# Earlier projections and adjacency reloads in four column parts, in a one-core graph kernel

## The chip, the cores and the metric

One core of one Trainium2 chip. Its engines are named as the profile names them: PE (TensorE, matmuls), PEld (TensorE's weight loads), DVE (VectorE), ACT (ScalarE), POOL (GpSimd) and SP (SyncE, which here only issues DMAs). Time is device time in microseconds (us). Lower is better.

## The reference

Two layers on 4096 nodes with 512 features. What matters of it:

```python
# layer 0
a = adj + eye(4096)
d = sum(a, axis=1) ** -0.5
out = relu((d[:, None] * a * d[None, :]) @ x @ W.T + b)
x = layernorm(x + out)
# layer 1: 8 heads, key size 64
q, k, v = x @ Wqs, x @ Wks, x @ Wvs            # per head
scores = q @ k.T / 8 + 0.01 * eye - 1e16 * (1 - max(adj, eye))
att = softmax(scores)
x = layernorm(x + sum over heads of (att @ v) @ Wo)
```

The adjacency matrix is 4096 x 4096 in float32 (64 MB). An off-diagonal entry is present with a chance of about 1/512, the diagonal is always present, and every present value is between 0.05 and 1.

## The kernel before, in words

Because all edges are below one and few, the kernel uses a short way: the mask of layer 1 leaves each node only itself, so layer 1 becomes one product with a combined weight `wvo`, and layer 0 becomes a gather over the few edges of a row. A test at the end (L1224) decides whether the short way held; if not, a general kernel follows. Only the short way, `few_edges_below_one`, runs here.

The rows are cut into NT = 32 tiles of 128. The work has two phases.

**Phase 1** (loop at L1049, steps t = 0 to 32) reads every adjacency tile once.

- SP loads adjacency tile t+3 (`load_first`, L561; `load_a`, L541). 14 tiles are "early" (0, 1, 3, 5, ... 25) and go with tiles 27 to 31 ("resident") into the pool `big` of five buffers `a_t`. The other 13 ("again": 2, 4, ... 26) pass through two buffers `a_n` and have to be read a second time in phase 2.
- ACT sums the rows of tiles that are not early (`sum_rows`, L710), or looks for negative entries in early ones (`sum_negative`, L715). POOL makes the degree factor `d_all` from the sum (`scaling`, L722 to L725).
- The projection x @ W.T of a tile: POOL issues the load of `x_t` (L550, five loads ahead, six buffers), PE transposes it (L689), ACT copies the transpose to `xT` (L694), PE multiplies with `wT` (`times`, L703) into one of five PSUM buffers `acc`. When the degree is known, ACT scales it (`keep_y`, L736) and POOL stores it to `y` in DRAM (L738).
- DVE scans adjacency tiles for their edges: per tile eight segments of 512 columns, each with one L752 (MAX8, the eight largest) and one L753 (their places). The function `some` (L986) advances this scan nine of its sixteen steps a tile per t. The order of tiles is early, resident, again (L560). Edges found are sorted (L756 to L838) and matched into nine slots (L844 to L900, with small steps on PE, ACT and DVE).

A list `due` (L1027 to L1032) holds, for each tile, the step in which `keep_y` runs. Step t begins with the projections whose due step lies between `lo` and `hi`:

```python
lo, hi = t + 1 + (t > EARLIER), t + 1 + (t >= EARLIER)      # L1058, EARLIER = NT - 7
ahead = [j for at, j in due if lo <= at <= hi]
```

So a projection runs one step ahead of its `keep_y`, and two steps ahead from t = 25 on.

**Phase 2** (loop at L1280) runs over output tiles i in the order of L560, nine slots k each.

- POOL gathers one row of `y` per node and slot (`gather`, L1110, an indirect DMA of 256 KB), 18 gathers ahead (L1099), in 19 buffers. The first gather needs all of `y`.
- For i > 0 the first two gathered buffers are added up by ACT (L1127) and DVE (L1129), called the presum below. PE multiplies each gathered buffer with a small matrix (L1316), nine products for i = 0 and eight for most others.
- DVE makes `h` from the result (`scaled`, L1180, and `residual`, L1188), which frees `yo` and `x_t` for the next `load_own` (L1115, SP). PE transposes `h` and multiplies it with `wvo`; ACT and DVE normalise it; ACT stores it (L1220).
- Between these, DVE scans the remaining tiles, shared out evenly (L1327). A tile of "again" is read a second time by `reload` (L994), called at k = 8 when a buffer is free: ACT must have looked through the old tile for negatives (`scan_half`, L1153, one half at k = 3 and one at k = 8) and DVE must have scanned it.

The order of the instructions on each engine is not the order of these lines: a scheduler reorders them. Only copies marked by `keep_in_program_order` (L696, L735) stay. Each engine, and SP's queue of DMA issues, then runs in its fixed order and waits in place.

Of the kernel before, what the change touches and what calls it, by code (L numbers as in the profile page):

```python
# [419 lines left out]
def few_edges_below_one(  # L420
# [21 lines left out]
    NT = N // P  # L442
# [33 lines left out]
    p1 = first.enter_context(tc.tile_pool(name="first", bufs=2))  # L476
# [64 lines left out]
    def load_a(t, pool=big, name="a_t", parts=1):  # L541
        a_t = pool.tile([P, N], FP, name=name)
        for c in range(parts):
            o = ts(c, N // parts)
            nc.sync.dma_start(a_t[:, o], adj[ts(t, P), o])
        return a_t
# [14 lines left out]
    def load_first(t, parts=1):  # L561
        if t in early or t in resident:
            return load_a(t, parts=2 if t == NT - 1 else parts)
        return load_a(t, pn, "a_n")

    a_tiles = {0: load_first(0, 4)}
# [8 lines left out]
    wT = p1.tile([P, ND, D], FP, name="wT", bufs=1)  # L575
# [25 lines left out]
    def load_second_weights():  # L601

        nc.sync.dma_start(
            wv.rearrange("p (h f) -> p h f", h=H),
            wvs.rearrange("h (p j) k -> p h (j k)", j=ND),
        )
        su1 = p1.tile([P, 2, ND, D], FP, name="wo", bufs=1)
        nc.sync.dma_start(su1[:, 0], wo.rearrange("(r a) k o -> (a k) r o", a=2))
        return su1

    def order_second_weights():
        nc.gpsimd.tensor_copy(
            w_nat.rearrange("p j (h k) -> p j h k", h=H),
            wv.rearrange("p (h j k) -> p j h k", h=H, j=ND),
        )
# [70 lines left out]
    def transpose_rows(src, dcs=range(ND)):  # L686
        pt = ps_t.tile([P, 512], FP, name="pt")
        for dc in dcs:
            nc.tensor.transpose(pt[:, ts(dc, P)], src[:, ts(dc, P)], ident)  # L689
        return pt  # L690

    def evacuate(pool, name, pt, pinned=False):
        dst = pool.tile([P, ND, P], FP, name=name, bufs=2)
        copy = nc.scalar.copy(dst.rearrange("p c s -> p (c s)"), pt[:, :D])  # L694
        if pinned:
            tc.keep_in_program_order(copy)  # L696
        return dst

    def times(srcT, w, u=None, dcs=range(ND)):
        if u is None:  # L700
            u = ps_a.tile([P, D], FP, name="acc")
        for dc in dcs:
            nc.tensor.matmul(  # L703
                u, srcT[:, dc, :], w[:, dc, :], start=(dc == 0), stop=(dc == ND - 1)
            )
        return u

    def sum_rows(dst, part):
        dump = wk_.tile([P, N], mybir.dt.uint8, name="dump")
        nc.scalar.activation(dump[:, : part.shape[1]], part, AF.Copy, accum_out=dst)  # L710

    def sum_negative(t, a_t, halves=(0, 1)):
        dump = wk_.tile([P, N], mybir.dt.uint8, name="dump")
        o = slice(halves[0] * N // 2, (halves[-1] + 1) * N // 2)
        nc.scalar.activation(  # L715
            dump[:, o], a_t[:, o], AF.Relu, scale=-1.0,
            accum_out=neg_all[:, t, halves[0] : halves[0] + 1],
        )

    def scaling(t, more=None):  # L720
        deg = small.tile([P, 1], FP, name="deg")
        nc.gpsimd.tensor_scalar(deg, deg_all[:, t : t + 1], 1.0, None, op0=ALU.add)  # L722
        if more is not None:
            nc.gpsimd.tensor_tensor(deg, deg, more, ALU.add)
        nc.gpsimd.tensor_tensor(d_all[:, t : t + 1], deg, mhalf, ALU.pow)  # L725

    def keep_y(t, u):
        if t in due_first:
            y_t = p1.tile([P, D], FP, name="y_t", bufs=4)
        else:  # L730
            if not y_bank:
                y_bank.append(p1.tile([P, 8, D], FP, name="wo", bufs=1))
            y_t = y_bank[0][:, y_count[0] % 8]
            y_count[0] += 1
        tc.keep_in_program_order(  # L735
            nc.scalar.activation(y_t, u, AF.Copy, scale=d_all[:, t : t + 1])  # L736
        )
        nc.gpsimd.dma_start(y[ts(t, P), :], y_t)  # L738
# [172 lines left out]
    def match(*stages):  # L911
        for stage in stages:
            n = staged[stage]
            if stage == KEY:
                ready = n < len(sorted_)
            elif stage == PERM:
                ready = n < staged[RANKS] and n - staged[MOVE] < 2
            else:
                ready = n < staged[stage - 1]
            if stage == ACROSS:  # L920
                ready = ready and n == staged[RANKS]
            if stage == MOVE:
                ready = ready and n == staged[END]
            if not ready:
                continue
            t = order[n]
            e = edges[t]
            if stage == KEY:
                e["key"] = match_key(t)
            elif stage == ACROSS:  # L930
                e["pk"] = match_across(e["key"])
            elif stage == RANKS:
                e["rank"] = match_ranks(e["key"], e["pk"])
            elif stage == PERM:
                e["perm"] = match_perm(e["rank"])
            elif stage == MOVE:
                e["pm"] = match_move(e["rec"], e["perm"])
            else:
                match_end(t, e["pm"])
                matched.add(t)  # L940
            staged[stage] += 1
# [44 lines left out]
    def some(upto):  # L986
        while count[0] < upto:
            count[0] += 1
            next(work, None)
# [4 lines left out]
    def reload():  # L994

        t = queue.pop(0)
        reloaded.append(t)
        a_tiles[t] = load_a(t)

    def spread(t, s_t, k, alone=False):  # L1000

# [21 lines left out]
    xs, us = {}, {}  # L1023
    DEEP = 3
    RATE = 9
    EARLIER = NT - 7
    due = [(t + 1, t) for t in range(NT) if t not in early]  # L1027
    for n, t in enumerate(early):
        at = max(t + 3, -(-STEPS * (n + 1) // RATE) + 1)
# [7 lines left out]
    def prefetch(count):  # L1037
        for _ in range(count):
            if fetch:
                t = fetch.pop(0)  # L1040
                xs[t] = load_x(t, nc.gpsimd, p1, 6)
# [7 lines left out]
    for t in range(NT + 1):  # L1049
        if t == 0:  # L1050
            su1 = load_second_weights()
        if t + DEEP < NT:
            a_tiles[t + DEEP] = load_first(t + DEEP)
        if t == 3:
            order_second_weights()
            setup = second_weights(su1)

        lo, hi = t + 1 + (t > EARLIER), t + 1 + (t >= EARLIER)  # L1058
        ahead = [j for at, j in due if lo <= at <= hi]
        pts = []  # L1060
        for j in ahead:
            prefetch(1)
            pts.append(transpose_rows(xs.pop(j)))
        kind, begin, end = next(setup, (None,) * 3) if len(ahead) < 2 else (None,) * 3
        got = begin() if kind == "t" else None
        if t < NT:
            if t in early:
                sum_negative(t, a_tiles[t])
            else:
                sum_rows(deg_all[:, t : t + 1], a_tiles[t][:, : N // 2 if t == NT - 1 else N])  # L1070
                more = None
                if t == NT - 1:
                    more = small.tile([P, 1], FP, name="more")
                    sum_rows(more, a_tiles[t][:, N // 2 :])
                scaling(t, more)
            if t in again:
                del a_tiles[t]
        if left:
            left()
            left = None  # L1080
        for j in [j for at, j in due if at == t]:
            keep_y(j, us.pop(j))
        for j, pt in zip(ahead, pts):
            us[j] = times(evacuate(p1, "xT", pt, t >= EARLIER), wT)
        if kind == "t":
            end(got)
        if kind == "p":
            left = lambda end=end, pa=begin(): end(pa)
        if t < NT - 5:
            match(*ALL)  # L1090
        some((t + 1) * RATE)
# [178 lines left out]
    def at(step, i, k):  # L1270

        near = {"T": (1, 5), "M": (1, 8), "Q": (2, 2), "V": (2, 3), "F": (2, 7)}
        far = {"T": (2, 0), "M": (2, 6), "Q": (3, 1), "V": (3, 4), "F": (3, 8)}
        for table, tiles in ((near, range(NT - 2, NT)), (far, range(NT - 2))):
            behind, place = table[step]
            if k == place and i - behind in tiles:
                return i - behind
        return None

    for i in range(NT + 2):  # L1280
# [6 lines left out]
        for k in range(KH):  # L1287
            ends = p == NT - 1
            t = at("T", i, k)
            if t not in (None, NT - 1):  # L1290
                hTs[t] = evacuate(p2, "hT", transpose_rows(hs[t]))
            t = at("M", i, k)
# [51 lines left out]
            t = at("Q", i, k)  # L1344
# [3 lines left out]
            t = at("V", i, k)  # L1348
# [4 lines left out]
            t = at("F", i, k)  # L1353
# [9 lines left out]
            if k == KH - 1 and queue and len(reloaded) < free:  # L1363
                reload()
# [34 lines left out]
```

## Time and profile before

| | |
|---|---|
| Time, median of 3 runs | 646.42 us (645.92 to 649.11) |
| The profiled execution's own time | 646.95 us |
| Span of its profile | 645.2 us |
| Granted TensorE clock, mean | 0.946 |
| PE, DVE, ACT, POOL busy | 545.8, 546.0, 504.6, 352.8 us |
| DMA | 217.68 MB, 337 GB/s on average |
| Last store of y issued (L738) | 223.43 us |
| First gather (L1110) | 226.55 us |
| First reload issued (L545) | 249.27 us |

The span is what the profiler recorded; the profiled execution's own time is 1.75 us longer, and 0.53 us above the median. Two of four engines are busy for 85% of the span, so the shares alone do not say which one ends the kernel; the stages have to be read one by one. A time in a row is the start in the span; "idle before" is idle time of that engine just before the instruction, with what ended it.

### The profile page before, as it was taken

Reading aid. Unit: us, or ns where it says so; the run is one execution under the profiler, and the core shown is the slowest. Engines: PE = TensorE matmul, PEld = TensorE weight load, DVE = VectorE, ACT = ScalarE, POOL = GpSimd, SP = SyncE. Lnnn points to the kernel's source line nnn. Section 1 sums busy time; section 2 is a strip of 40 time slices with the busy share of each in tenths; the row PEclk is TensorE's granted clock in tenths of the full one; section 3 lists DMA queues with packets and bytes.
Section 4 is the critical chain, followed back from the end, with each engine's and each line's share of the span. In section 5 each row is a group of like instructions: output and inputs, shape, how many; then the busy total and the mean of one; then the engine's idle time right before and its main releaser. Section 6 shows DMA issues by size and latency. Waiting matters only on the chain. (4 is left out here: it accounts for less than half of the span.)

```text
span 645.2 us, 7918 instructions
## 1 busy us (share of the span) xinstructions
PE 545.8 (85%) x1579; PEld 251.2 (39%) x1579; DVE 546.0 (85%) x2143; ACT 504.6 (78%) x1114; POOL 352.8 (55%) x465
## 2 busy tenths in 40 slices
PE   1699876488979756799898898999999999999993
PEld 1354332233434222344343343444444444444352
DVE  5699999999999995998899999999999995431521
ACT  1868667786988957699989877889988998986543
POOL 5222223223342377676776767767677777777700
PEclk9899987788979968799899998999999999999998
DMA  9999999799999388999999999999998888888721
GB/s 331 402 421 421 424 428 423 286 422 424 423 425 419 157 270 284 400 351 385 387 408 409 401 401 387 305 348 348 328 362 280 269 263 300 281 285 276 238 70 54
DMA packets 51515, 217.68 MB, mean 337 GB/s; under 512 B 8062, under 2 KB 9086, under 8 KB 45441
## 3 DMA queue, kind: packets, MB, share of 16 engines
q1 hardware_dynamic: 18128, 115.35, 44.7%
q0 software_dynamic: 28192, 92.30, 41.0%
q10 hardware_dynamic: 5136, 9.44, 3.9%
q14 instruction: 45, 0.36, 0.2%
q8 instruction: 14, 0.23, 0.1%
HBM read 200.28 MB, written 16.78 MB: 336 GB/s over the span
## 5 line engine op out<-in xcount | busy, mean ns | idle before, releaser
L1110 POOL DMA_INDIRECT g<-y,cols_all x288 | 282.5, 981 | 107.1 <-issue 43.1
L1316 PE MATMUL acc<-g,s_t 128*128 128x512 f32 x482 | 232.0, 618 | 28.0 <-DVE g L1129 17.1
L752 DVE MAX8 v_all<-a_t 128x8 f32<-128x512 f32 x256 | 166.3, 677 | 8.2 <-DMA a_t<-in_adj_dram 8.2
L753 DVE FIND_INDEX8 idx<-v_all,a_t 128x8 uint32<-128x512 f32 x256 | 173.0, 683 | 0.0
L703 PE MATMUL acc<-wT,xT 128*128 128x512 f32 x256 | 128.9, 658 | 31.4 <-ACT xT L694 31.3
L1316 PEld LDWEIGHTS acc<-g,s_t 128*128 128x128 f32 x482 | 89.8, 196 | 125.9 <-issue 95.1
L703 PE MATMUL acc<-wvo,hT 128*128 128x512 f32 x256 | 117.6, 601 | 4.5 <-ACT hT L694 3.8
L715 ACT ACTIVATE dump<-a_t 128x2048 uint8<-128x2048 f32 (+1 forms) x50 | 119.1, 2382 | 0.0
L703 PEld LDWEIGHTS acc<-wT,xT 128*128 128x128 f32 x256 | 52.1, 211 | 95.6 <-issue 59.1
L703 PEld LDWEIGHTS acc<-wvo,hT 128*128 128x128 f32 x256 | 48.6, 192 | 65.1 <-issue 57.0
L1007 ACT ACTIVATE sq<-cols,wr_all 128x128 f32<-128x128 f32 x160 | 58.7, 394 | 0.2
L1011 ACT ACTIVATE s_t<-sq,wr_all 128x128 f32<-128x128 f32 x128 | 58.2, 486 | 0.7 <-ACT sq L1007 0.2
L722 POOL TENSOR_SCALAR deg<-deg_all 128x1 f32<-128x1 f32 x32 | 7.1, 224 | 83.3 <-DVE deg_all L971 48.8
L1129 DVE SCALAR_TENSOR_TENSOR g<-g,wr_all 128x512 f32<-128x512 f32 x37 | 27.5, 743 | 25.5 <-ACT g L1127 22.7
L710 ACT ACTIVATE dump<-a_n 128x4096 uint8<-128x4096 f32 x13 | 47.3, 3636 | 0.0
L550 POOL DMA_DIRECT2D x_t<-in_x_dram x32 | 18.0, 566 | 46.3 <-PE pt L689 37.6
L1127 ACT ACTIVATE g<-g,wr_all 128x512 f32<-128x512 f32 x31 | 22.1, 713 | 24.0 <-DMA g<-y,cols_all 16.8
L783 DVE MAX8 top<-key 128x8 f32<-128x64 f32 x192 | 36.0, 213 | 0.3
L1180 DVE SCALAR_TENSOR_TENSOR h<-yo,own_all,acc 128x512 f32<-128x512 f32 (+1 forms) x33 | 23.8, 720 | 11.2 <-PE acc L1316 7.8
L1020 ACT ACTIVATE s_t<-s_t,wr_all 128x128 f32<-128x128 f32 x92 | 33.0, 391 | 0.0
L694 ACT COPY hT<-pt 128x512 f32<-128x512 f32 x31 | 18.0, 579 | 16.4 <-PE pt L689 15.4
L694 ACT COPY xT<-pt 128x512 f32<-128x512 f32 x32 | 18.3, 594 | 11.5 <-PE pt L689 11.5
(134 smaller groups left out, 676.8 us busy)
## 6 DMA issues: line engine op xcount, KB each, us to landing
a_t<-in_adj_dram SPq DMA_DIRECT2D x30, 2048.0 KB, 15.3
a_n<-in_adj_dram SPq DMA_DIRECT2D x13, 2048.0 KB, 13.6
x_t<-in_x_dram POOLq DMA_DIRECT2D x32, 256.0 KB, 12.6
yo<-y SPq DMA_DIRECT2D x32, 256.0 KB, 6.6
x_t<-in_x_dram SPq DMA_DIRECT2D x32, 256.0 KB, 5.9
out_dram<-r_t ACTq DMA_DIRECT2D x32, 256.0 KB, 5.2
y<-y_t POOLq DMA_DIRECT2D x18, 256.0 KB, 13.6
g<-y,cols_all POOLq DMA_INDIRECT x288, 6.3
```

Of the source, the lines that this page charges most:

```text
L694: copy = nc.scalar.copy(dst.rearrange("p c s -> p (c s)"), pt[:, :D])
L703: nc.tensor.matmul(u, srcT[:, dc, :], w[:, dc, :], start=(dc == 0), stop=(dc == ND - 1))
L710: nc.scalar.activation(dump[:, : part.shape[1]], part, AF.Copy, accum_out=dst)
L715: nc.scalar.activation(dump[:, o], a_t[:, o], AF.Relu, scale=-1.0, accum_out=neg_all[:, t, halves[0] : halves[0] + 1],)
L752: long.append(lambda o=o, seg=seg: nc.vector.max(v[:, o], seg))
L753: long.append(lambda o=o, seg=seg: nc.vector.max_index(idx[:, o], v[:, o], seg))
L783: return lambda: nc.vector.max(top[:, f, r * 8 : r * 8 + 8], keyf[:, f])
L1007: nc.scalar.activation(sq, cols1, AF.Square, bias=wr[:, 2, k : k + 1])
L1011: nc.scalar.activation(s_t[:, k, :], away(), AF.Relu, scale=wr[:, 3, k : k + 1], bias=wr[:, 1, k : k + 1],)
L1020: nc.scalar.activation(s_t[:, k, :], s_t[:, KH, :], AF.Copy, scale=wr[:, 1, k : k + 1])
L1110: nc.gpsimd.indirect_dma_start(out=slots[j], out_offset=None, in_=y[:, :], in_offset=bass.IndirectOffsetOnAxis(ap=cols_all[:, t, k : k + 1 ...
L1316: nc.tensor.matmul(zs[i], mats[i][:, KH if k < summed[i] > 1 else k, :], slots.pop(i * KH + k), start=False, stop=(k == KH - 1),)
```

## The change

Two edits. First, the projections' lead over `keep_y` grows in three steps: two steps from t = 17, three from t = 21, four from t = 25, where it had been one, and two from t = 25. The mark `keep_in_program_order` on the copy to `xT` stays where it was (t >= 25). Worked out from the list `due`, the projections run in these steps:

| step t | 17 | 18 | 19 | 20 | 21 | 22 | 23 | 24 | 25 | 26 | 27 | 28 | 29 | 30 |
|---|---|---|---|---|---|---|---|---|---|---|---|---|---|---|
| before | 15 | 18 | 17 | 20 | 19 | 22 | 21 | 24 | 23, 26 | 25, 27 | 28 | 29 | 30 | 31 |
| after | 15, 18 | 17 | 20 | 19 | 22, 21 | 24 | 23 | 26 | 25, 27, 28 | 29 | 30 | 31 | - | - |

Second, a reload is issued as four DMAs of 1024 columns (512 KB) each instead of one of 2048 KB. 13 reloads become 52 DMAs.

```diff
@@ reload
-        a_tiles[t] = load_a(t)
+        a_tiles[t] = load_a(t, parts=4)
@@ before the loop of phase 1
-    EARLIER = NT - 7
+    SOONER = (17, 21, 25)
+
+    def projected(t):
+
+        return t + 1 + sum(t >= e for e in SOONER)
+
@@ in the loop of phase 1
-        lo, hi = t + 1 + (t > EARLIER), t + 1 + (t >= EARLIER)
+        lo, hi = projected(t - 1) + 1, projected(t)
         ahead = [j for at, j in due if lo <= at <= hi]
...
-            us[j] = times(evacuate(p1, "xT", pt, t >= EARLIER), wT)
+            us[j] = times(evacuate(p1, "xT", pt, t >= NT - 7), wT)
```

`load_a` (L541) already has the argument: it makes one `dma_start` per part, each into its own columns of the same buffer, so that a reader of the first columns waits for the first part alone.

## Prediction, made before the changed kernel ran

> **What bounds the kernel now.** I read the digit lines first: DVE, ACT and DMA all stand near 9 through phase 1, PE through the second half. Shares do not decide between them, so I cut the span at the places where one of them changes, and read these stages:
>
> ```profile
> core 0: us, PE busy (x) PEld busy (x) DVE busy (x) ACT busy (x) POOL busy (x), PEclk, DMA share, GB/s
> 150.00:200.00 50.00, 42.70 (x114) 20.32 (x115) 50.00 (x129) 42.07 (x39) 18.08 (x39) 0.90 1.01 424
> 226.00:249.00 23.00, 11.31 (x20) 4.64 (x21) 22.98 (x93) 15.82 (x44) 17.27 (x18) 0.72 0.82 254
> 249.00:257.00 8.00, 7.96 (x16) 3.09 (x14) 0.22 (x2) 4.23 (x13) 5.87 (x8) 0.85 0.91 333
> 257.00:300.00 43.00, 37.56 (x104) 16.36 (x104) 40.33 (x172) 36.26 (x93) 29.14 (x30) 0.92 0.99 375
> 300.00:345.00 45.00, 38.18 (x112) 16.93 (x112) 43.23 (x204) 42.56 (x116) 31.71 (x33) 0.96 1.02 400
> 345.00:398.00 53.00, 47.22 (x141) 21.14 (x142) 53.00 (x242) 45.52 (x131) 38.03 (x38) 1.00 1.02 402
> 398.00:500.00 102.00, 101.35 (x301) 45.58 (x301) 100.71 (x455) 87.85 (x259) 74.95 (x75) 0.98 0.95 330
> 500.00:602.00 102.00, 101.09 (x303) 45.27 (x301) 61.35 (x247) 88.37 (x259) 76.96 (x80) 1.00 0.85 275
> ```
>
> From 398 on PE is full (202.4 of 204 us): what PE gains before 398 the end gains, and nothing else does. From 300 to 398 DVE is full, and PE's waits there (11.7 us, six times) all end with L1129, the presum. In phase 1 DVE is full too, and stays so until 249. Only from 249 to 257 DVE does nothing. The timelines of DVE, PE and POOL around it:
>
> ```profile
> 223.43 0.54 POOL L738 DMA_DIRECT2D y<-wo  x1 [0.42 <-ACT wo L736]
> 226.55 1.07 POOL L1110 DMA_INDIRECT g<-y,cols_all  x1 [2.58 <-DMA y<-wo]
> ...
> 232.94 10.51 PE L1316 MATMUL acc<-g,s_t 128*128 128x512 f32 x18 [10.95 <-DMA x_t<-in_x_dram]
> ...
> 247.51 0.74 DVE L1129 SCALAR_TENSOR_TENSOR g<-g,wr_all 128x512 f32<-128x512 f32 x1
> ...
> 248.78 0.44 DVE L873 TENSOR_SCALAR perm<-sources,rank 128x640 bf16<-128x640 bf16 x1
> 257.00 0.75 DVE L1180 SCALAR_TENSOR_TENSOR h<-yo,own_all,acc 128x512 f32<-128x512 f32 x1 [7.78 <-PE acc L1316]
> ...
> 260.90 1.28 DVE L752 MAX8 v_all<-a_t 128x8 f32<-128x512 f32 x2
> ...
> 265.93 0.73 DVE L1129 SCALAR_TENSOR_TENSOR g<-g,wr_all 128x512 f32<-128x512 f32 x1
> ```
>
> The presum of tile 1 (247.51) stands behind DVE's own backlog of scanning, whenever the gathers come. After 249.2 DVE has no tile to scan: the first reload is issued at 249.27 and lands 11.0 us later, and the scan starts at once (260.90). Until then DVE waits for the eight products of tile 1. Two more views, the waits of 226 to 275 and the DMA queues of 252 to 259:
>
> ```profile
> ACT g L1127 <- DMA g<-y,cols_all: 10.3, 2, 6.1
> DVE h L1180 <- PE acc L1316: 7.8, 1, 7.8
> ...
> q1 hardware_dynamic: 225, 2.24, 79.9%
> q0 software_dynamic: 136, 0.46, 16.4%
> ```
>
> The first says that the gathers are late for ACT too at the start of phase 2. The second: while the reload (q1) runs, it gets five times what the gathers (q0) get, and gathers that took 3.7 us to land take 9.7.
>
> **Part 1, the earlier projections.** No instruction is added; the `x_t` loads, transposes, copies and products of 15 tiles move forward by one or two steps, and up to three more projections stand finished in PSUM. At the end of phase 1 ACT waits 2.68, 1.75 and 0.61 us for PE's projections; these go. The last adjacency half lands at 213.7 (issue 190.91 plus 22.8). ACT's 1.91 + 0.18, POOL's 0.19 + 0.57, ACT's 0.67 and the store (0.54 + 2.58) then allow the first gather at about 220.5: at most 6 us earlier, I take 5. Of itself this is worth nothing: DVE, never idle from 25 to 249, still reaches L1129 at 247.51. Price of the move: three more `x_t` (0.75 MB, 1.8 us at the 424 GB/s of that stage) go through the DMA queues before adjacency tile 27, which lands at 187.6 (171.30 plus 16.3) and is scanned from 190.50. The margin of 2.9 us covers it; without it, up to 1 us would fall on DVE. POOL's loads pass its degree steps, but POOL is idle for two thirds of that stage. In the built order, three projections instead of two stand on PE ahead of the last match of phase 1, and DVE's reader (L893, at 150) is itself moved back by 3.7 us of other work, about one projection: 0, at worst 2.
>
> PE's idle time between tile 0 and tile 1 grows from 4.75 to about 10 us. By the row, tile 1 already ran at a clock of 0.85 (8.65 us for 16 records, where 6 records at full clock take 2.74). [...] Row: 0; [...] Neither is on the path here, since the changed order reads tile 1's result only at about 264.
>
> What the earlier gathers do buy is ACT's 10.3 us. ACT then enters 275 to 325, where it is full, with less left to do. I expect its late results to go: DVE's 0.71 (L1129 at 273.49) and 1.92 us (L873 at 294.25), PE's 0.83 and 0.34 (rank_key).
>
> **Part 2, the reload in parts.** After L873 at 248.8, DVE's built order now has 19 instructions ahead of tile 1's L1180: the scan's first five MAX8 and five FIND_INDEX8, eight small ones, and the presum of tile 2; 8.1 us by their own durations. So DVE waits for the first quarter in place of tile 1. SP issues it at the same 249.27, for it stands behind the `yo` and `x_t` loads that DVE's L1180 and L1188 release. The bytes of the reload move from about 252.5 to 259.5. A quarter takes 1.8 us if q1 keeps its share, 2.6 if smaller packets bring it down to even with q0; with 1.3 from the last byte to the scan (259.6 to 260.90) DVE starts between 255.5 and 256.5. I take 255.8: idle 6.6 instead of 7.78, 1.2 saved. Later quarters arrive at the rate at which two segments are scanned (2.5 us).
>
> The other twelve reloads gain nothing, for DVE waits for none of them: the one wait list entry DVE <- a_t (8.2 us) is the start of the kernel. Their price: 39 more issues at 0.4 us on SP, which mostly waits; reload 2's parts 2 to 4 now stand behind `yo` and `x_t` of tile 4 until about 266 and should land near 274, when two segments are being scanned from part 1. Packets become 4 KB. [...] The trace has several DMAs in flight here: from 300 to 390, q0 (4 KB packets) spends 50.3% of the engines on 17.45 MB, q1 46.1% on 16.76 MB, 5% more per byte, which is 0.25 us a reload. I take the row: 3 us in all, under the slack of DVE's scan. If that cover failed, about nine reloads lie in the full stage: 2 us.
>
> **What the new order costs.** The scheduler made new orders throughout phase 2. Adding DVE's durations by kind along both orders, the presum of tile 5 comes 3.1 us of work later, those of tiles 6 to 14 come 1.2 to 1.9 later; at tile 12, the last before PE is full (397.0), 1.55.
>
> **Sum**, at the presum of tile 12: -1.2 (quarter), -0.71 and -1.92 (ACT), +1.55 (order): -2.3. PE can follow: tile 2's products start at 262.4 instead of 266.7, with two products of L703 moved behind them (1.9 to 3.8), and PE's 1.17 gone. PE's wait at 469.9 (0.65, DVE) may add a little: -2.5. The profiled execution's 646.95 becomes 644.4; it stood 0.53 above the median, so 643.9 against 646.42.
>
> **Rivals.** (a) Slower: the first quarter is late. DVE now stands in front of it with the presum of tile 2 behind. If the scan starts at time T, the sum above is zero at T = 258.1, and at 255.5 if ACT's 2.63 us stay. For: [...] the packets shrink to a quarter. Against: `yo` and `x_t` are drained by 252.5. With T = 259 and ACT's waits kept, 3.6 us slower: 650.0. (b) No gain: T near 256, ACT's waits replaced by others (it stays 95% full from 300 to 345), order +1.55: 646.5. (c) More: T near 254, all waits gone, and part of PE's 11.7 us too because the clock no longer drops (two half-clock stretches, 316 and 398, follow such waits): 5 to 6 us, 641.
>
> **How the numbers follow.** A difference under 0.5% (3.2 us) is what a measurement of this kernel cannot tell from none. Forecast 0.40 (642.5 to 645.5), (a) 0.22, (b) 0.20, (c) 0.18. Faster by more than that is (c) and a third of the forecast, 0.33; slower is most of (a), 0.19; the rest 0.48. The range leaves out about half of (a) and a third of (c): 640 to 650.
>
> **What would show it.** Right: first gather near 221; DVE busy without a gap up to 249, then 6 to 7 us idle ended by a DMA of a_t at L752; presum of tile 2 at 261 to 262; no wait of ACT for g after 250; PE full from 395. Wrong: DVE waits before 249; a wait for a_t at a later reload; PE gaps of 300 to 398 as long as before or longer.

## The result, and the profile after

| | before | after |
|---|---|---|
| Time, median of 22 runs each on the same chip | 647.47 us (645.76 to 651.88) | 648.25 us (645.0 to 651.0) |
| Ratio after to before, 95% interval | | 1.001 (0.9993 to 1.0026) |
| The profiled execution's own time, and its span | 646.95 and 645.2 us | 646.88 and 645.0 us |
| First gather | 226.55 us | 228.82 us |
| Start of the first reload's scan (L752) | 260.90 us | 257.44 us |
| Presum of tile 9, of tile 12 | 357.26, 396.95 us | 354.80, 397.80 us |

The difference is within what a measurement of this kernel can tell from none. The forecast was 643.9 us with a range of 640 to 650; what came has the size of rival (b), no gain. Ratios here and below compare fast runs alone, those within 1.5% of the fastest of the same kernel; where the runs of a kernel scatter by more, as in e14 (12 of 22 counted), the median of all runs lies nearer to the kernel before (0.9986 instead of 0.9942).

In the kernel after, lines from L1027 on are five higher: the presum is L1134, the gather L1115, PE's product L1321, the out store L1225. All experiments below have the line numbers of the kernel before.

The stages of the kernel after, in the columns used before:

```profile
core 0: us, PE busy (x) PEld busy (x) DVE busy (x) ACT busy (x) POOL busy (x), PEclk, DMA share, GB/s
249.00:257.00 8.00, 6.26 (x11) 2.30 (x9) 0.39 (x1) 6.51 (x21) 5.96 (x7) 0.79 0.92 306
345.00:398.00 53.00, 47.66 (x136) 21.01 (x133) 49.86 (x227) 45.17 (x129) 36.38 (x38) 0.94 1.03 395
398.00:500.00 102.00, 101.13 (x300) 45.44 (x301) 100.63 (x454) 89.87 (x265) 73.81 (x75) 0.98 0.96 340
```

DVE still does nothing from 249 to 257. It is no longer full from 345 to 398 (49.86 of 53 us, where it had 53.00). PE is full from 398 on, as before. So two things have to be explained: why the early part brought little, and what DVE waited for after 345.

The end of phase 1, from the timelines of PE, ACT and POOL:

```profile
201.37 1.02 PE L689 MATMUL pt<-ident,x_t 128*128 128x128 f32 x4 [2.06 <-DMA x_t<-in_x_dram]
...
199.35 0.58 ACT L694 COPY xT<-pt 128x512 f32<-128x512 f32 x1 [2.48 <-PE pt L689]
...
202.49 0.58 ACT L694 COPY xT<-pt 128x512 f32<-128x512 f32 x1 [1.97 <-PE pt L689]
202.97 3.62 ACT L710 ACTIVATE dump<-a_t 128x4096 uint8<-128x4096 f32 x1
...
210.82 0.58 ACT L694 COPY xT<-pt 128x512 f32<-128x512 f32 x1 [2.99 <-PE acc L703]
...
228.82 1.07 POOL L1115 DMA_INDIRECT g<-y,cols_all  x1 [2.59 <-DMA y<-wo]
```

PE has been ordered to transpose earlier and waits for `x_t`, which is not there: such waits come four times (174.70 to 205.11), 8.4 us in all. ACT starts nothing else while a copy waits. Two copies to `xT` (199.35 after 2.48 us, 202.49 after 1.97 us) now stand ahead of the degree sum of tile 28 (L710, 202.97), and a third (210.82 after 2.99 us) ahead of the next one; together they wait 7.4 us. The degree sums come late, and with them the last `y`.

The start of the first reload's scan, from DVE's timeline of the kernel after:

```profile
257.44 1.29 DVE L752 MAX8 v_all<-a_t 128x8 f32<-128x512 f32 x2 [7.38 <-DMA a_t<-in_adj_dram]
...
263.12 0.74 DVE L1134 SCALAR_TENSOR_TENSOR g<-g,wr_all 128x512 f32<-128x512 f32 x1
```

And its DMA queues from 252 to 259 (packets, MB, share of the engines):

```profile
q1 hardware_dynamic: 456, 1.59, 63.6%
q0 software_dynamic: 248, 0.83, 31.9%
```

DVE waits for the first quarter now, 7.38 us in place of 7.78 for tile 1's products. The gathers (q0) get a third of the traffic of that stretch where they had a sixth, and the reload (q1) lands later (the last quarter at 264.2, the whole reload before at 260.3). What changed for q1 is its packets: on average 10 KB before (2.24 MB in 225), 3.5 KB now, about as large as the 3.3 KB of q0; by the sizes in the trace those of the reload went from 16 KB to 4 KB. Whether this is why the gathers get more was not tested alone; e10 and e11, with the same four parts, show similar shares (65.8 to 34.4% and 61.5 to 33.8%).

What happens after 345. First the presums of tiles 9 and 12 in the kernel before:

```profile
357.26 0.75 DVE L1129 SCALAR_TENSOR_TENSOR g<-g,wr_all 128x512 f32<-128x512 f32 x1
...
396.95 0.75 DVE L1129 SCALAR_TENSOR_TENSOR g<-g,wr_all 128x512 f32<-128x512 f32 x1
```

The same in the kernel after, with what ACT, PE and DVE wait for in between:

```profile
354.80 0.75 DVE L1134 SCALAR_TENSOR_TENSOR g<-g,wr_all 128x512 f32<-128x512 f32 x1
...
359.89 0.34 ACTq L1225 DMA_DIRECT2D out_dram<-r_t  x1
360.27 0.69 ACT L1007 ACTIVATE sq<-cols,wr_all 128x128 f32<-128x128 f32 x2 [2.84 <-DMA a_t<-in_adj_dram]
362.01 0.09 DVE L786 MATCH_VALUE_LOAD key<-top,key 128x8 f32 x1 [0.93 <-ACT mask L805]
...
369.48 0.48 PE L856 MATMUL pt<-ident,rank_key 128*128 128x128 f32 x1 [2.75 <-ACT rank_key L849]
...
375.59 0.69 ACT L1007 ACTIVATE sq<-cols,wr_all 128x128 f32<-128x128 f32 x2 [2.85 <-DMA a_t<-in_adj_dram]
376.15 0.19 DVE L893 COPY wr_all<-pt 128x27 f32<-128x27 f32 x1 [2.13 <-PE pt L885]
...
397.80 0.75 DVE L1134 SCALAR_TENSOR_TENSOR g<-g,wr_all 128x512 f32<-128x512 f32 x1
```

At tile 9 the presum is 2.46 us ahead of before. Then ACT stands still (2.84 and 2.85 us; six such waits from 316 to 388, 13.2 us in all: five are put down to a DMA of `a_t`, one to one of `x_t`). L1007 reads neither: the wait belongs to the out store just ahead of it (L1225, issued at 359.89 and 375.20). The trace names the semaphore that each DMA reports its landing to. The DMAs of SP and ACT share eight of them, 23 or 24 DMAs each. The store of 359.89 has the semaphore of a quarter that SP issued 17.5 us earlier (from the view of L545 in the kernel after, from 342.3 to 342.5):

```profile
L545 SPq DMA_DIRECT2D a_t<-in_adj_dram x1: 327/327/327, 342.4 to 342.4; - x1
...
  ACT sq L1007: 2.8, 1
...
DMA to landing us min/median/max: 17.4/17.4/17.4
```

342.4 plus 17.4 is 359.8, and the store follows. In each of the six waits the store is issued 0.08 us after the landing of the DMA that had its semaphore last. In the kernel before, with whole reloads, that landing lies 10.9 us or more ahead of the store for all eight stores from 300 to 398. In e10 below, with the later reloads whole, it lies 10 us or more ahead for seven of the eight; for the eighth the trace does not tell. ACT's mask and rank are late behind these waits, PE waits 2.75, DVE waits 0.93 and 2.13. At tile 12 the presum is 0.85 us behind before.

ACT was not free of waits before the change either. In the kernel before it waited in the same stretch for PE's transposes, and once 2.6 us for DVE:

```profile
ACT hT L694 <- PE pt L689: 7.4, 6, 2.2
```

So its waits from 300 to 398 grew from 10.0 to 13.2 us. What is new is less their sum than what stands behind them: the mask and the rank for which DVE and PE wait.

### The profile page after: what moved, and what is told of

Same layout as the page of the kernel before. It is cut to its first block, busy times and chain, and to the rows that moved or that the text cites. A ratio compares the mean times of both kernels' runs of the same rounds, so it can differ in the third digit from the quotient of the medians.

```text
span 645.0 us, 7974 instructions
## 1 busy us (share of the span) xinstructions
PE 544.6 (84%) x1579; PEld 250.6 (39%) x1579; DVE 546.3 (85%) x2143; ACT 504.6 (78%) x1114; POOL 352.9 (55%) x465
## 5 line engine op out<-in xcount | busy, mean ns | idle before, releaser
L1115 POOL DMA_INDIRECT g<-y,cols_all x288 | 282.5, 981 | 104.7 <-issue 44.7
L1321 PE MATMUL acc<-g,s_t 128*128 128x512 f32 x482 | 234.5, 622 | 29.5 <-DMA x_t<-in_x_dram 14.6
L752 DVE MAX8 v_all<-a_t 128x8 f32<-128x512 f32 x256 | 166.4, 680 | 15.4 <-DMA a_t<-in_adj_dram 15.4
L703 PE MATMUL acc<-wT,xT 128*128 128x512 f32 x256 | 124.1, 638 | 25.8 <-ACT xT L694 25.7
L1321 PEld LDWEIGHTS acc<-g,s_t 128*128 128x128 f32 x482 | 89.8, 197 | 128.9 <-issue 88.9
L703 PE MATMUL acc<-wvo,hT 128*128 128x512 f32 x256 | 115.7, 594 | 1.4 <-ACT hT L694 0.8
L703 PEld LDWEIGHTS acc<-wT,xT 128*128 128x128 f32 x256 | 50.6, 204 | 87.6 <-issue 57.0
L1007 ACT ACTIVATE sq<-cols,wr_all 128x128 f32<-128x128 f32 x160 | 58.6, 393 | 13.4 <-DMA a_t<-in_adj_dram 11.5
L1134 DVE SCALAR_TENSOR_TENSOR g<-g,wr_all 128x512 f32<-128x512 f32 x37 | 27.5, 744 | 23.6 <-ACT g L1132 17.9
L710 ACT ACTIVATE dump<-a_n 128x4096 uint8<-128x4096 f32 x13 | 47.2, 3634 | 0.0
L783 DVE MAX8 top<-key 128x8 f32<-128x64 f32 x192 | 36.2, 214 | 0.3
L689 PE MATMUL pt<-ident,x_t 128*128 128x128 f32 x128 | 20.2, 292 | 10.6 <-DMA x_t<-in_x_dram 8.4
```

Source lines behind the costliest of these rows:

```text
L703: nc.tensor.matmul(u, srcT[:, dc, :], w[:, dc, :], start=(dc == 0), stop=(dc == ND - 1))
L752: long.append(lambda o=o, seg=seg: nc.vector.max(v[:, o], seg))
L783: return lambda: nc.vector.max(top[:, f, r * 8 : r * 8 + 8], keyf[:, f])
L1007: nc.scalar.activation(sq, cols1, AF.Square, bias=wr[:, 2, k : k + 1])
L1115: nc.gpsimd.indirect_dma_start(out=slots[j], out_offset=None, in_=y[:, :], in_offset=bass.IndirectOffsetOnAxis(ap=cols_all[:, t, k : k + 1 ...
L1134: nc.vector.scalar_tensor_tensor(g, slots.pop(i * KH + k), w, g, op0=ALU.mult, op1=ALU.add)
```

## The experiments

Two theories stood at the start. A: the earlier projections gain and the parts take it back through ACT's waits at the out store. B: neither edit reaches PE's chain. The runs fell on chips of two kinds: on one the kernel before takes about 647 us, on the others about 720 us. Each ratio is to the kernel before on the same chip, run beside it. On the 720 us chips phase 1 runs as in the profiles shown so far, but phase 2 does not (see the last section), so times in phase 2 from those chips are compared with each other only. e14 and e18 are one kernel on two chips and differ by 0.6%, so ratios from different chips that differ by no more than that are not told apart.

| run | kernel | before, us | ratio, 95% interval |
|---|---|---|---|
| e1, e16 | projections alone | 720.28, 720.01 | 1.0065 (1.0028 to 1.0101), 1.0045 (1.0019 to 1.0072) |
| e2, e13 | parts alone | 720.28, 720.01 | 0.9925 (0.989 to 0.9959), 0.9894 (0.9837 to 0.9951) |
| e6 | both (the change) | 721.15 | 0.9989 (0.9964 to 1.0013) |
| e9 | projections up to three steps, no parts | 721.15 | 0.9989 (0.9968 to 1.001) |
| e11 | projections up to three steps, parts | 647.23 | 0.9977 (0.9958 to 0.9996) |
| e10 | only the first reload in parts | 647.23 | 1.0002 (0.9982 to 1.0023) |
| e3 | both, out store by SP | 720.28 | 0.9934 (0.9898 to 0.997) |
| e14, e18 | as e11, out store by SP | 720.01, 722.45 | 0.9942 (0.9909 to 0.9975), 1.0004 (0.998 to 1.0028) |
| e4, e15 | first reload before the gathers | 720.28, 720.01 | 0.9874 (0.9824 to 0.9924), 0.9815 (0.9764 to 0.9866) |
| e17 | as e9, first reload before the gathers | 722.45 | 0.9916 (0.9878 to 0.9953) |
| e7 | parts, first reload before the gathers | 721.15 | 1.008 (1.0049 to 1.011) |
| e8 | as e7, out store by SP | 721.15 | 1.0146 (1.0097 to 1.0194) |
| e12 | nine gathers ahead | 647.23 | 1.0376 (1.0309 to 1.0443) |

**Each edit alone, and both** (e1 and e16, e2 and e13, e6).

```diff
 # projections alone (e1, e16)
-        a_tiles[t] = load_a(t, parts=4)
+        a_tiles[t] = load_a(t)
 # parts alone (e2, e13): the kernel before with
-        a_tiles[t] = load_a(t)
+        a_tiles[t] = load_a(t, parts=4)
```

> The earlier projections alone, each reload one DMA. Theory A (the two edits cancel: the projections relieve ACT and DVE, the parts take it back through ACT's waits for DMAs at the out store): the waits of ACT at L1007 behind the out store (13.2 us from 300 to 398 in the changed kernel) are gone, PE is full from about 396, 644 to 645.5 us. Theory B (no edit reaches PE's chain; new waits stand where old ones went, whatever the reloads do): ACT's waits at the out store gone as well, but PE full from 397.5 to 399 as in both kernels, 646 to 648 us. Both: the first gather is again near 229 (2 us later than before), and DVE is idle for 7 to 11 us near 249 to 260, now ended by the whole reload or by tile 1's products.

> The earlier projections alone, each reload one DMA, where the kernel before runs in 647 us. First gather at 228 to 229.5. DVE has tiles to scan up to 249 whatever the gathers do, so if the late first gather is hidden there: 0.997 to 1.001. If it comes through by tile 1's products, for which DVE waits at 249: their end moves from 257 to 259 or later, and the ratio is 1.002 to 1.005. Where the kernel before runs in 720 us: 1.003 to 1.010 again.

> The reloads in four parts alone, projections as before. Theory A: the first gather is back at 226.5, the first quarter lands near 257, ACT's waits for a_t and x_t DMAs at the out store add up to 8 us or more from 300 to 398, and with ACT's three gather waits of before still there the time is 648 to 650 us. Theory B: ACT's waits are there but PE is full from 397 to 399: 646 to 648 us.

> The reloads in four parts alone, projections as before, on whatever chip: where the kernel before runs in 647 us, only the later twelve reloads differ from the run with the first reload alone in parts (1.0002). If ACT's waits for quarters at the out store hold up the chain: they are there (8 to 11 us from 300 to 398) and the ratio is 1.001 to 1.005. If they cost nothing: 0.998 to 1.001. Where the kernel before runs in 720 us: 0.989 to 0.996 again.

> The changed kernel itself, on a chip of the kind that runs the kernel before in 720 us, with the experiments beside it. If the two edits simply add up (+0.65% for the projections and -0.75% for the parts, measured alone): a ratio of 0.996 to 1.002, so that the out store by SP, at 0.993 with both edits, is worth 0.4 to 0.8% by itself. If ACT's waits at the out store cost nothing here: 0.991 to 0.995, the same as with the store by SP, and the edits do not add up. First gather between 228 and 231 by both.

The projections alone are slower and the parts alone faster, both against theory A, on two chips (e1 and e2 ran on one, e16 and e13 on another). The products of the single ratios are 1.0065 x 0.9925 = 0.9990 and 1.0045 x 0.9894 = 0.9939; for both edits together 0.9989 was measured, on a third chip. So on these chips the change is a loss and a gain that about cancel. The loss goes with a later end of phase 1: the first gather is at 229.82 and 229.97 with the projections alone, at 225.07 and 225.72 with the parts alone. 4.7 us of 720 are 0.65%. The gain goes with the first reload: with parts alone its scan starts 5.4 us after the first issue (269.67, 275.06), with the projections alone 13.7 us after (272.82, 286.48). ACT's waits at the out store do not appear with the parts on these chips (none in e2 and e13; in e6 one gap of 1.8 us ahead of a store, for which the trace knows no releaser). In e2 SP issues the four parts of a reload within 2.0 us (from 339.75), so its semaphores seem to be free in time there. In the change the third part comes 5.6 us after the first (342.39 and 347.98), 0.02 us after the landing of the quarter that had its semaphore last (347.96). e13 and e16 were to show how the single edits weigh where the kernel takes 647 us, but fell on a 720 us chip too. No run on a 647 us chip has one edit alone, so for the comparison that the forecast was about, the split stays open.

**One step less of lead** (e9 with whole reloads, e11 with parts).

```diff
-    SOONER = (17, 21, 25)
+    SOONER = (17, 21)
```

> The projections' lead ends at three steps (two from t = 17, three from t = 21, no fourth at t = 25), each reload one DMA. If it is the last step of the lead that puts copies waiting for x_t ahead of the degree sums: ACT's waits at L694 from 185 to 215 fall from 8.0 us (four, in the kernel with all three steps) to under 4, and the first gather comes at 225 to 227, as before the change or 2 us later, not at 229.8; ratio 0.997 to 1.003 instead of 1.0065. If the earlier steps already do it (the x_t loads from t = 21 on queue behind adjacency tiles): first gather at 228.5 to 230, ratio 1.004 to 1.008.

> The changed kernel without the last step of the projections' lead (two steps from t = 17, three from t = 21), all reloads in four parts. If the last step of the lead is what costs (0.9989 without it against 1.0065, each with whole reloads) and the parts are worth their 0.75% beside it: 0.989 to 0.994, first gather at 225 to 226. If the changed kernel's 0.9989 is not made of these two terms: 0.996 to 1.001.

The end of phase 1 of e11, from the timelines of ACT and POOL:

```profile
199.50 0.58 ACT L694 COPY xT<-pt 128x512 f32<-128x512 f32 x1 [2.48 <-PE pt L689]
199.98 3.62 ACT L710 ACTIVATE dump<-a_t 128x4096 uint8<-128x4096 f32 x1
...
204.73 0.59 ACT L694 COPY xT<-pt 128x512 f32<-128x512 f32 x1
...
224.76 1.07 POOL L1110 DMA_INDIRECT g<-y,cols_all  x1 [2.59 <-DMA y<-wo]
```

The copy that stood at 202.49 ahead of the sum of tile 28 now stands behind it (204.73) and no longer waits. The sum starts at 199.98 instead of 202.97, the next one at 205.20 instead of 211.31, the last one is done 4 us earlier, and the first gather is at 224.76 (225.69 in e9). PE's waits for `x_t` are the same as in the change (2.06 at 201.52, 2.76 at 205.23). So here the loads do not come earlier for being wanted earlier; the fourth step of lead only puts ACT's copies, waiting for them, ahead of one more degree sum each. e11 is the one version that is faster than before on a 647 us chip, by 0.23% (its interval ends at 0.9996), less than the 0.5% that counts here. e9's part of the expectation on ACT's waits was wrong: they fell only from 8.0 to 7.1 us. Which sum they stand ahead of mattered, not their length.

**More loads of x_t under way** (e5, one run of each: 730.73 us beside 720.83).

```diff
-    x_t: 6 buffers, prefetch(5); y_t: 4 buffers
+    x_t: 8 buffers, prefetch(7); y_t: 2 buffers
```

> The earlier projections alone, with eight x_t buffers and seven loads ahead instead of six and five (two y_t buffers instead of four pay for it). If it is the x_t loads that hold the earlier projections up at the end of phase 1: PE's waits for DMA x_t at L689 from 170 to 215 (8.4 us, four times, in the changed kernel) fall to under 3 us, ACT's waits of 2.5, 2.0 and 3.0 us at the xT copies go, and the first gather comes at 222 to 225.5 instead of 228.8. If the DMA engines' total bytes set that end (they are full to about 215 in every order): the waits move to the adjacency tiles, the last of which lands later, and the first gather stays at 226 to 229. The time is within 0.5% of the kernel with the earlier projections alone by both, since DVE is full to 249 whenever the gathers come.

PE's waits at L689 from 170 to 215 are gone, but the first gather is at 237.75. DVE now waits for adjacency tiles (0.99 us at 187.00, 2.76 at 200.00), as the second case of the expectation had it, and ACT waits 9.6 us at 166 for a `y_t` buffer, which the experiment itself took away. So the run does not separate the two, and whether the queue or the number of loads ahead holds `x_t` up stays open.

**The first reload alone in parts** (e10).

```diff
-        a_tiles[t] = load_a(t)
+        a_tiles[t] = load_a(t, parts=4 if len(reloaded) == 1 else 1)
```

> Only the first reload in four parts, the other twelve whole, projections as before. If the gain of the parts (0.9925 with all reloads in parts) is the earlier start of the first reload's scan alone, which is what DVE waits for: the scan starts 5 to 6 us after the first issue, and the ratio is 0.990 to 0.995. If the later reloads carry it: 0.997 to 1.002.

This run was on a 647 us chip, so it does not answer for the gain of parts on the others. It does show the later reloads' part. The waits of 300 to 398 (us in total, times, longest) in the kernel after:

```profile
ACT sq L1007 <- DMA a_t<-in_adj_dram: 11.5, 5, 2.8
...
PE pt L856 <- ACT rank_key L849: 4.3, 4, 2.8
```

The same view of e10, in which there is no row of ACT waiting for a DMA:

```profile
PE pt L856 <- ACT rank_key L849: 0.2, 1, 0.2
```

And the presum of tile 12 in DVE's timeline of e10:

```profile
395.10 0.75 DVE L1129 SCALAR_TENSOR_TENSOR g<-g,wr_all 128x512 f32<-128x512 f32 x1
```

With the later reloads whole, ACT has no wait at its stores and PE waits 0.2 us for ranks instead of 4.3. At tile 9 e10 is 1.8 us ahead of before (355.50), and it still is at tile 12. The change and e11, which both cut the later reloads, have the waits (11.5 and 11.3 us) and lose 3.3 and 1.8 us between tiles 9 and 12. DVE's wait for the first quarter was 6.78 us, 1.0 less than before; the median over 22 runs does not show it (1.0002, the interval reaches 1.2 us down).

Two things limit what these profiles say of the time. The profiled executions of e10 (644.14 us) and e11 (644.35) are among the fastest of their 22, 3.4 and 1.6 us under their medians. And a lead at tile 12 did not decide the rest: e10 has the presum of tile 12 1.8 us before e11 (396.89), but at tile 15 the two are level:

```profile
443.44 0.73 DVE L1129 SCALAR_TENSOR_TENSOR g<-g,wr_all 128x512 f32<-128x512 f32 x1
```

That is e10; in e11 it starts at 443.40. Near 400 e10 has a stretch of lower clock (0.77 from 393 to 400, a loss of 1.6 us) and e11 has none (1.00), see the last section. In the median e11, with the waits, is ahead of e10, without them.

**The out store by SP** (e3, and with a lead of three steps e14 and e18).

```diff
-        nc.scalar.dma_start(out[ts(order[i], P), :], r_t)
+        nc.sync.dma_start(out[ts(order[i], P), :], r_t)
```

> Both edits, the out store issued by SP instead of ACT, so ACT issues no DMA in phase 2. Theory A: ACT's 13.2 us of waits from 300 to 398 go, PE's waits of 2.75 (369) and 0.81 (397) for rank_key and DVE's 0.93 and 2.13 go with them, PE is full from 395 to 396.5, 644.5 to 646 us; SP now waits at the stores instead, and a reload behind one comes up to 2 us later, for which DVE has slack. Theory B: ACT's waits go and PE's presum waits stay: 646.5 to 648.5 us.

> The changed kernel without the last step of the lead (0.9977), and the out store issued by SP. If ACT's waits at the out store (9.1 us before it) hold up the ranks and with them PE and DVE: ACT's waits and PE's 2.64 us for rank_key at 370 go, PE is full from 395 to 396.5 instead of 397.7, 0.993 to 0.996. If not: 0.997 to 0.999, or above where reloads wait behind stores on SP.

> The changed kernel without the last step of the lead, and the out store issued by SP. Where the kernel before runs in 647 us (0.9977 with the store on ACT): if ACT's 9 us of waits at the out store hold up the chain, they and PE's 2.64 us for rank_key at 370 go and the ratio is 0.993 to 0.996; if not, 0.997 to 1.000. Where the kernel before runs in 720 us: 0.992 to 0.997 again.

0.9934, 0.9942 and 1.0004: the same kernel gave the last two, so these ratios show no gain of the store by SP. All fell on 720 us chips, where ACT hardly waits at the store anyway. What ACT's waits cost where they occur was not measured by this.

**The first reload before the gathers** (e4, e15; e17, e7, e8 with other edits).

```diff
     load_own(1)
+    scan_half(); scan_half(); reload()
```

> Neither edit. The two negative checks of tile 27 and the first reload (one DMA) are moved ahead of the gathers, before the phase 2 loop. If DVE's idle 7.8 us at 249 to 257 bounds the stage up to 398 (DVE full there): first reload issued near 233 to 238 instead of 249.27, landed by about 247, DVE without a gap over 2 us from 226 to 260, PE full from 391 to 395 instead of 398, 640 to 644.5 us. If PE's chain of 257 to 398 is bound by something else (PE's own 123 us of work in 141, ACT 95% full): DVE's gap moves to later waits, 645.5 to 647.5 us. Slower than 648 only if the reload delays the 18 gathers and with them tile 1's products by more than 5 us.

> Neither edit; the first reload moved ahead of the gathers, where the kernel before runs in 647 us. If DVE's 7.8 us at 249 to 257 are on the way to the end: they go, PE is full from 391 to 394, 0.990 to 0.994. If the products of tile 1 and the ranks set the pace instead, DVE waits later for what it did not wait for before: 0.997 to 1.002. Where the kernel before runs in 720 us: 0.983 to 0.992 again.

> The lead of the projections ends at three steps, reloads whole, and the first reload moved ahead of the gathers. Where the kernel before runs in 647 us: if DVE's idle time at 249 to 257 is on the way to the end, it goes and the ratio is 0.988 to 0.993; if tile 1's products and the ranks set the pace, 0.996 to 1.000. Where the kernel before runs in 720 us: the early reload gave 0.987 and 0.982 alone and the three steps 0.9989, so 0.980 to 0.988.

> Reloads in four parts and the first reload moved ahead of the gathers, projections as before. If the two fill different idle time of DVE (later reloads by the parts, 249 to 257 by the early one): their ratios multiply, 0.9925 x 0.9874 = 0.980, 0.977 to 0.983. If both fill the same hole, the wait for the first reload: 0.986 to 0.990, no better than the early reload alone.

> As the kernel with parts and the early reload, and the out store issued by SP. If ACT's waits at the out store hold PE up: 0.4 to 0.8% below the kernel without this step. If not: the same within 0.3%; above it by up to 0.5% if SP's waits at the stores hold up reloads.

The first reload is issued at 227.26 (e4) and DVE is busy for 23.00 of 23 us to 249 and for 6.19 of the next 8. The two runs of it alone, 0.9874 and 0.9815 (six executions each), are the lowest ratios of the study; on these chips they beat the kernel before, and the change (0.9989 on another such chip) by more than the 0.6% between chips. With parts it is slower than before (e7, e8): there DVE's built order puts short operations ahead of the reload's scan, these start one at a time with gaps of up to 4 us, and the scan starts at 265.71 instead of 246.43. None of the five fell on a 647 us chip, so what the early reload brings there is open.

**Nine gathers ahead** (e12).

```diff
-    AHEAD = 18
+    AHEAD = 9
```

> Neither edit; nine gathers ahead instead of eighteen, so the burst of gathers at the start of phase 2 is half as long. In the runs at 720 us DVE's short operations start about once per gather (1.25 us) while POOL issues the burst, and MAX8 and FIND_INDEX8 do not wait. If it is the gathers' issue on POOL that holds DVE: DVE's waits without a releaser between the first gather and tile 1's presum fall from over 10 us to under 6, the presum of tile 1 comes 5 us or more earlier, and later tiles lose some of it to late gathers (ratio 0.985 to 1.01). If it is something else (the traffic of the gathers' data, code loading): the waits stay where they were.

It was on the 647 us chip, where DVE has no waits without a releaser to begin with, so its question stays unanswered. What it shows, in two executions, is the price of late gathers, 3.8%.

## Why the prediction was wrong

Two steps failed. The first in time is the end of phase 1. The prediction took away ACT's waits for projections and then counted the chain of degree sums after the last adjacency half: first gather 5 us earlier, 221. It came 2.3 us later. The prediction did count the `x_t` loads as bytes but not as something to wait for. e9 and e11 show the place: the last step of lead costs about 4 us, and with it gone the first gather is at 224.8 to 225.7, against 225.1 to 226.6 in the runs with the projections of before. What the other two steps bring, if anything, is lost in that spread. By the prediction's own account this step was worth nothing by itself, and on the 647 us chip that held.

The step that failed in the sum is the later reloads: the twelve that "gain nothing" were given a price of 3 us, "under the slack of DVE's scan", and so put at nothing. At tile 9 the presum was 2.46 us ahead, near the 2.3 of the sum, which the prediction expected to last to tile 12. There it was 0.85 us behind, and between the two DVE waited 0.93 and 2.13 us for results that ACT's waits at the out store had made late.

Point by point:

- **The first gather is worth nothing by itself.** Held where the kernel takes 647 us: DVE was full to 249, tile 1's presum was at 247.35 (before 247.51), and PE started tile 1's products at 248.15 (before 248.31). It did not hold on the 720 us chips, where 4.7 us of the first gather went along with 0.45 to 0.65% of the time.
- **ACT's 10.3 us of waits for gathers.** They were two, 6.09 and 4.24 us; one of 5.66 is left, for the first gathers were not earlier. Still DVE's two late results, 0.71 at 273 and 1.92 at 294, went. The larger one is gone in e10 too, where the projections are those of before, so that term came true by luck.
- **The quarter.** Taken as T = 255.8; it was 257.44 (255.67 in e10, 256.84 in e11). It saved 0.4 us of DVE's wait, not 1.2, and a further wait of 0.97 us came ahead of it. Rival (a) was right in kind, as DVE does stand in front of the quarter, and not in size. SP's four parts overlapped: they were issued from 249.12 to 250.53 and landed at 257.42, 259.01, 261.49 and 264.16, the last one 3.9 us after the whole reload of before.
- **The new order.** Taken as 3.1 us at tile 5 and +1.55 by tile 12. The presum was 2.81 us ahead at tile 2, 0.80 behind at tile 5, 2.46 ahead at tile 9: a lead was made, lost by the order (DVE has no wait from 257 to 360), and made again. DVE's busy time from 226 to 398 is the same (159.8 and 160.2 us). That the sum came out at tile 9 is partly luck. The prediction called DVE full from 300 to 398, but its own row has 43.23 of 45 us there: a wait of 1.77 us (L893 at 320.69). It went as well, uncounted, and made up for the 0.8 us that the quarter fell short and the 0.97 ahead of it.
- **The later reloads.** "Gain nothing" held, DVE waits for none. The price that came was on ACT: the prediction looked at SP's queue and at the DMA engines, but not at what the additional DMAs do to the completion semaphores that ACT's own stores share. DVE's two waits between tiles 9 and 12 ended with results that came late from ACT, directly or through PE. That the later parts bring ACT's waits and PE's waits for ranks is shown by e10 beside the change and e11. That they cost the missing gain in the median is not shown: e10's presum kept its lead to tile 12 and its median did not, and e11 has the waits and the lower median.
- **DVE's waits as a sum.** From 226 to 398 they were 12.2 us, and were to fall by 3.8; they are 11.4. Rival (b) said it of ACT: waits replaced by others.
- **PE's idle time before tile 1.** It was to grow from 4.75 to about 10 us, at no cost by the row. The first gather was late, and the idle time fell to 2.60 us, so what a longer idle time costs was not shown.
- **PE full from 395.** It was from 398.6.
- **Right as well:** DVE has no wait before 249, so neither the additional `x_t` loads nor the moved match cost it anything.

## What to carry to other kernels

To run work earlier, look first at what it waits for: here the order asked for `x_t` before it had landed, PE stood for 8.4 us and ACT's copies for 7.4, and the degree sums behind them paid (that of tile 28 started at 202.97, in e11 at 199.98). Cutting a DMA into parts adds DMAs, so look at every engine that issues DMAs of its own: in this program SP and ACT share eight completion semaphores, and six of ACT's stores waited 13.2 us for SP's loads. And follow one due time, here the presum, tile by tile through the span; the two traces agree at the end though a lead of more than 2 us was made and lost twice on the way.

## What the runs showed of the hardware that was not expected

**DVE can stand still while POOL issues gathers, on some chips.** Timeline of POOL and DVE in e1, on a 720 us chip:

```profile
251.24 0.95 POOL L1110 DMA_INDIRECT g<-y,cols_all  x1 [0.30 <-DMA g<-y,cols_all]
252.42 0.23 DVE L774 SCALAR_TENSOR_TENSOR key<-v_all,key 128x64 uint32<-128x64 uint32 x1 [3.85 <-remote]
...
253.76 0.95 POOL L1110 DMA_INDIRECT g<-y,cols_all  x1 [0.30 <-issue]
...
255.21 0.29 DVE L774 SCALAR_TENSOR_TENSOR key<-v_all,key 128x128 f32<-128x128 f32 x1 [2.56 <-remote]
```

While POOL issues gathers without a break, every 1.25 us, DVE's short operations start one at a time, 1.2 to 3.9 us apart, with no releaser that the trace knows. In e1 such waits, for which the trace names no engine and no DMA of this core, come to 50 us from 226 on; before and after the change on a 647 us chip they are 0 and 0.3 us, with gathers of the same 0.95 us. MAX8 at L783, which by the expectation of e12 does not wait, was held as well (up to 1.7 us). What holds DVE, and why one chip shows it and another does not, no run tested, since e12 fell on the other kind of chip. This stays open.

**Half clock after one short wait and not after another.** From 398 to 500 the granted clock was 0.98 before and after and 1.00 in e11; PE's last wait before its full stage was 2.08 us before, 1.24 after and 1.94 in e11. In e10, with a wait of 2.13, it was 0.77 from 393 to 400. The window just behind that wait, in the kernel after (the columns are those of the stages):

```profile
400.00:407.00 7.00, 7.00 (x18) 2.79 (x18) 5.79 (x23) 3.98 (x16) 4.73 (x5) 0.80 1.02 383
```

And in e11:

```profile
400.00:407.00 7.00, 7.00 (x22) 3.12 (x21) 7.00 (x27) 4.59 (x15) 3.89 (x5) 1.00 1.00 356
```

0.80 over 7 us, with 0.96 over the 7 us before it, is a loss of 1.7 us (the clock is at 0.50 from 399.4 to 402.8): 0.26%, where 2.5 us were forecast. A single profile of each kernel cannot tell that from an effect of the change.
